# Sink attention: the order of scores, dense products and weighing in a cycle of two units, and the split of the PSUM banks

## The chip, the cores and the metric

The kernel runs on one core of a Trainium2 chip. The core has a matrix engine (TensorE, PE in the profile), three engines for elementwise work (VectorE or DVE, ScalarE or ACT, GpSimd or POOL), a queue for transfers (SyncE or SP), and the accumulation memory PSUM, into which PE writes. The kernel uses PSUM as eight banks of 128 x 512 floats. The metric is the device time of one execution in microseconds; the median of three executions is 4220.33 us (4219.34 to 4223.46).

## The reference

The program computes sixteen blocks of a small hybrid network, each of them as `x = x + block(layernorm(x))`, over 16 sequences of 256 tokens with 128 channels. The change lies in one of them, attention with a sliding window of 128 tokens and a "sink": an extra score per head that takes part in the softmax but carries no value. Cut to what matters:

```
h = layernorm(x);  n = rmsnorm(h, scale)
q = rope(n Wq + bq), k = rope(n Wk + bk)    # 16 query heads, 4 key heads, 64 wide
v = n Wv + bv
scores = q . k where |pos_q - pos_k| <= 128, else a very low number
probs = softmax([scores, sink]) without the last column
h = h + (probs v) Wo + bo
```

The kernel doesn't take the maximum away before the exponential. So a head's output is (sum of exp(score) v) / (sum of exp(score) + exp(sink)), and everything in it is a matrix product, an exponential, a mask, or a division. A mixture of experts follows in the same block.

## The kernel before

The stage is `window_attention` of the class `Fast` (from line 3190). The 4096 tokens are eight chunks of 512, each holding two sequences of 256. A unit of the attention is (chunk c, side, sequence b, query tile it, key tile jt), with tiles of 128 tokens and a side being half of the heads; there are 8 x 2 x 2 x 2 x 2 = 128 units, and two neighbours with jt = 0 and 1 make the weighted sums of one query tile. What happens to unit n:

- `score(n)` (line 3249) takes two score banks, `self.bank("s")`, and issues two matmuls of 512 columns on PE, one on SBUF rows 0 to 63 and one on rows 64 to 127. ACT takes the exponential of both banks into the tile `pt` (128 x 1024).
- `masked(n)`: where it and jt differ, DVE multiplies `pt` with the mask `far`. For jt = 1, POOL adds the pair's two `pt` tiles to `both`, from which the denominators come.
- `weigh(n, slot)` (line 3272): for each unit, eight matmuls `pt` x `v` of 128 rows by 32 columns into four quarters of the bank `po`; for jt = 1 also four matmuls of ones x `both` into the bank `pd`, the denominators. Each of these lines' matmuls leaves two records in the trace.
- `inverse`: ACT takes the logarithm of `pd` plus the sink's exponential, in two halves, and then exp of its negative, which is the reciprocal `rd`. The two logarithms release `pd`.
- `divide`: DVE multiplies `po` with `rd` into `ot`, and so releases `po`.

Around this, the same loop issues dense products on PE, with the full 128 x 128 array: `prepare` projects q, k and v of the next side (eight slots ahead of its first unit; each roped projection is read from PSUM by two DVE instructions, then shuffled by DVE and added by POOL at the next step), `out` is the output projection of four matmuls, and `before` and `after` are the norms of the next and the last chunk. From the second chunk on the norms have a compact form, in which line 1798 makes four small matmuls of 128 rows by 32 columns, ACT takes two functions of the result, and SP sends the rows out with four small transfers. Each dense product takes one bank of the tag "s" and gives it back when DVE or ACT has read it.

The order is written out by hand (`manual_schedule`), by a loop over slots n. Every slot has one score unit. An even slot goes on with dense products (`prepare`, `out`, `before`, `after`), an odd slot with `weigh` of the units n - 3 and n - 2. A dictionary `due` holds what is deferred to the beginning of a later slot, after the slot's score: `masked(n)` in slot n + 1, `inverse` in the slot after its weighing, `divide` one later, and the `peak` reductions of DVE.

`share` splits the eight PSUM banks among tags; a tag's banks are used in turn, and an allocation waits until the bank's last user is read out. Before, four banks are "s" (scores and dense products together) and four are "o" (`po` and `pd` in turn).

Of the kernel before, what the change touches and what calls it, by code (L numbers as in the profile page):

```python
# [1649 lines left out]
class Fast(Net):  # L1650
# [1539 lines left out]
    def window_attention(self, w, h, n1, ns2):  # L3190
# [3 lines left out]
        with ExitStack() as st:  # L3194
# [7 lines left out]
            units = [(c, side, b, it, jt) for c in range(NCH) for side in range(2) for b in range(2) for it in range(2) for jt in range(2)]  # L3202
            qs, ks, vs, pts, ots, sums, both, due = {}, {}, {}, {}, {}, {}, {}, {}
# [19 lines left out]
            def later(slot, f, *args):  # L3223
                due.setdefault(slot, []).append((f, args))

            def prepare(i, step, slot):

                c, side = divmod(i, 2)
                s = self.chunk(c)
                while pending:  # L3230
                    moved()
                if step == 0:
                    qs[i] = p2.tile([P, 4, CH], F32, tag="q", name="q")
                    ks[i] = p2.tile([P, CH], F32, tag="k", name="k")
                    roped("k", side, s, ks[i])
                    later(("last", slot + 4), self.peak, WINDOW + side, 1, c, ks[i])
                for g in ((0,), (1, 2), (3,), ())[step]:
                    roped("q", 4 * side + g, s, qs[i][:, g])
                    later(("last", slot + 4), self.peak, WINDOW + side, 0, 4 * c + g, qs[i][:, g])
                if side == 0 and step > 1:  # L3240
                    pv = self.bank("s")
                    v = p1.tile([P, 2, T], F32, tag="v", name="v", bufs=4)
                    for k in range(2):
                        t = 2 * step - 4 + k
                        self.mm(pv[:, k * T : k * T + T], n1[:, c * CH + t * P : c * CH + t * P + P], w["Wv"])
                        vs[c, t] = v[:, k]
                    self.tt(v, self.bt(pv), w["bv"][:, None, :].broadcast_to([P, 2, T]), ALU.add)

            def score(n):
                c, side, b, it, jt = units[n]  # L3250
                i0, j0 = b * T + it * P, b * T + jt * P
                q, k = qs[2 * c + side], ks[2 * c + side]
                pt = p2.tile([P, 2, 4, P], F32, tag="pt", name="pt", bufs=6)
                ps = [self.bank("s"), self.bank("s")]
                for half in range(2):
                    rows = slice(64 * half, 64 * half + 64)
                    self.mm(ps[half].rearrange("p (h t) -> p h t", h=4), k[rows, j0 : j0 + P], q[rows, :, i0 : i0 + P])
                for half in range(2):
                    self.act(pt[:, half].rearrange("p h t -> p (h t)"), ps[half], AF.Exp)
                pts[n] = pt  # L3260
# [11 lines left out]
            def weigh(n, slot):  # L3272
                c, side, b, it, jt = units[n]
                if jt == 0:
                    sums[0] = self.bank("o"), self.bank("o")
                pt = pts.pop(n)
                po, pd = sums[0]


                for dh in range(3 if jt else 2):  # L3280
                    if dh == 2:
                        pt = both.pop(n)
                    for r in range(4):
                        half, hh = divmod(r, 2)
                        d = (2 * side + half) * 64 + 32 * dh
                        at = dh % 2 * T
                        nc.tensor.matmul(
                            (pd if dh == 2 else po)[32 * r : 32 * r + 32, at : at + T],
                            self.ones64[:, :32] if dh == 2 else vs[c, 2 * b + jt][:, d : d + 32],
                            pt[:, half, 2 * hh : 2 * hh + 2].rearrange("p h t -> p (h t)"),  # L3290
                            start=dh == 2 or (jt == 0 and dh == 0), stop=dh == 2 or (jt == 1 and dh == 1), skip_group_check=True,
                        )
                if jt:
                    later(slot + 1, inverse, n, po, pd, slot + 2)
# [19 lines left out]
            def out(i):  # L3314
                c, side = divmod(i, 2)
                pz = self.bank("s")
                ot = ots.pop(i)
                for g in range(4):
                    at = (4 * side + g) * C
                    self.mm(pz, w["Wof"][:, at : at + C], ot[:, g], start=g == 0, stop=g == 3)  # L3320
                hs = h[:, self.chunk(c)]
                if side:
                    self.tt(hs, hs, pz, ALU.add)
                else:
                    self.stt(hs, pz, w["bo"], hs, ALU.add, ALU.add)
# [3 lines left out]
            def before(c, i):  # L3329

                s = self.chunk(c)
                if i == 0:
                    held["sq"] = self.centre_step(p1, self.x[:, s], h[:, s], "s", square=True)
                elif i == 1:
                    held["rs"] = self.spread_step(p1, held["sq"], "s", twice=True, compact=c > 0)
                else:
                    r1, r2 = held["rs"]
                    self.stt(n1[:, s], h[:, s], w["ns1"], r2, ALU.mult, ALU.mult)
                    self.tt(h[:, s], h[:, s], r1, ALU.mult)

            def after(c, i):

                s = self.chunk(c)
                if i == 0:
                    held["sq"] = p1.tile([P, CH], F32, tag="nsq", name="nsq", bufs=2)
                    self.act(held["sq"], h[:, s], AF.Square)
                elif i == 1:
                    held["rs"] = self.spread_step(p1, held["sq"], "s", compact=c < NCH - 1)
                else:
                    self.stt(n1[:, s], h[:, s], ns2, held["rs"], ALU.mult, ALU.mult)  # L3350

            with self.share(s=4, o=4), self.tc.manual_schedule():
                self.logs()
                for n in range(-14, len(units) + 16):
                    if 0 <= n < len(units):
                        score(n)
                        later(n + 1, masked, n)
                    for f, args in (*due.pop(n, []), *due.pop(("last", n), [])):
                        f(*args)
                    if n % 2:  # L3360
                        for i in (n - 3, n - 2):
                            if 0 <= i < len(units):
                                weigh(i, n)
                        continue
                    i, step = divmod(n + 8, 8)
                    if 0 <= i < 2 * NCH:
                        prepare(i, step // 2, n)
                    i, rest = divmod(n - 14, 8)
                    if rest == 0 and 0 <= i < 2 * NCH:
                        out(i)  # L3370
                    c, u = divmod(n + 16, 16)
                    if c == 0 and u in (2, 4, 6):
                        before(c, u // 2 - 1)
                    if u in (0, 2, 6) and 0 < c < NCH:
                        before(c, (u + 1) // 3)
                    c, u = divmod(n - 24, 16)
                    if u in (0, 2, 6 if c < NCH - 1 else 4) and 0 <= c < NCH:
                        after(c, (u + 1) // 3 + (u == 4))
# [497 lines left out]
```

## Time and profile before

| | |
|---|---|
| median of three runs | 4220.33 us |
| profiled execution | 4218.15 us, its span 4216.4 us |
| PE busy, whole span | 3831.5 us (91%) |
| DVE, ACT, POOL busy, whole span | 2551.0, 2281.8, 1853.7 us |
| this stage, from its first projection to its last products | about 2881.9 to 3347 us from the span's start |
| one chunk of the stage in its steady part | 56.6 us |
| PE, DVE, ACT, POOL busy in it | 56.60, 45.47, 28.16, 31.29 us |

How to read it: one execution is recorded by the hardware profiler. A row of the timeline gives the start from the span's start, the length of the merged instructions, the engine, the line of the kernel, the operation, "what it writes <- what it reads", the shape, and how many records were merged; brackets give the idle time of the engine before it and what ended it. Most matmuls are issued in a helper at line 504, so the tiles' names tell them apart: `ps<-q,k` is a score, `ps<-hb,w`, `ps<-w,hb` and `ps<-ot,w` are dense products, `ps<-pt,v` of line 3287 is the weighing and `ps<-both,ct` the denominators. The shape before the sizes (64\*128, 128\*128, 128\*32) is the part of the array that the matmul uses. The ends of matmuls are modelled by the profiler, so starts are the safer reading.

### The profile page before, as it was taken

The page shows a single profiled execution, that of the slowest core. Times are in us where ns is not written, and L with a number is a line of the kernel's source. Part 1 is how long each engine was busy: PE and PEld are TensorE (multiplying, and loading weights), DVE is VectorE, ACT ScalarE, POOL GpSimd, SP SyncE. Part 2 cuts the span into 40 slices and gives each one's busy share as a digit, 9 for nine tenths or more (in the row PEclk, how much of TensorE's full clock was granted, in tenths as well). Part 3 has the DMA queues.
Part 4 walks back from the last instruction along what each step waited for, and adds up shares of the span by engine and source line. Part 5 has one row for each costly group of instructions (what it writes and reads, how often), then busy time and mean ns, then how long its engine had stood idle before and what let it go on. Part 6 is the DMA issues. An engine that isn't in the chain of part 4 may idle for free. (4 is left out here: it accounts for less than half of the span.)

```text
span 4216.4 us, 74153 instructions
## 1 busy us (share of the span) xinstructions
PE 3831.5 (91%) x29030; PEld 2182.7 (52%) x29030; DVE 2551.0 (61%) x4503; ACT 2281.8 (54%) x4478; POOL 1853.7 (44%) x1632
## 2 busy tenths in 40 slices
PE   7999999998899999985989869888999999899978
PEld 3555466464455466454965459543444344455333
DVE  4776576374577477473346633556877676486474
ACT  6665466555766466652457634444554454774532
POOL 4754365232565166225433434454555455321251
PEclk8999999998999999996999979999999999999979
DMA  1800000000000000004920058100000000000000
GB/s 61 347 15 12 11 9 9 22 1 1 20 11 14 6 7 9 6 11 142 323 69 12 17 182 295 41 19 21 16 14 16 8 0 10 7 2 19 6 0 21
DMA packets 110086, 190.88 MB, mean 45 GB/s; under 512 B 16126, under 2 KB 70788, under 8 KB 109600
## 3 DMA queue, kind: packets, MB, share of 16 engines
q1 hardware_dynamic: 97248, 162.83, 11.7%
q0 software_dynamic: 9120, 18.51, 1.3%
q8 instruction: 231, 3.78, 0.4%
q10 hardware_dynamic: 3360, 4.72, 0.3%
q14 instruction: 127, 1.04, 0.1%
HBM read 118.28 MB, written 54.20 MB: 41 GB/s over the span
## 5 line engine op out<-in xcount | busy, mean ns | idle before, releaser
L528 ACT ACTIVATE pt<-ps 128x512 f32<-128x512 f32 x640 | 339.5, 600 | 337.5 <-PE ps L504 336.2
L504 PE MATMUL ps<-hb,w 128*128 128x512 f32 (+1 forms) x960 | 463.7, 617 | 3.9 <-issue 3.3
L504 PE MATMUL ps<-w,hb 128*128 128x512 f32 (+2 forms) x896 | 405.2, 573 | 27.3 <-DVE t L531 18.5
L534 POOL TENSOR_TENSOR t<-t,t 128x512 f32<-128x512 f32 x256 | 319.9, 1271 | 153.7 <-DVE t L531 107.8
L531 DVE TENSOR_TENSOR t<-ps,tab 128x512 f32<-128x512 f32 x512 | 317.5, 681 | 70.1 <-ACT sq L528 66.7
L534 POOL TENSOR_TENSOR t<-t,ss 128x1024 f32<-128x1024 f32 x128 | 243.7, 1904 | 195.2 <-ACT ss L528 194.0
L504 PEld LDWEIGHTS ps<-hb,w 128*128 128x128 f32 (+1 forms) x960 | 179.6, 191 | 261.8 <-issue 220.6
L528 ACT ACTIVATE qkt<-ps 128x512 f32<-128x512 f32 x256 | 140.6, 595 | 299.2 <-PE ps L508 299.2
L531 DVE TENSOR_TENSOR u<-u,ps 128x384 f32<-128x384 f32 (+1 forms) x206 | 121.8, 595 | 277.2 <-ACT u L528 114.9
L534 POOL TENSOR_TENSOR nsq<-ha 128x512 f32<-128x512 f32 x112 | 123.2, 1100 | 354.3 <-ACT ha L528 342.3
L531 DVE TENSOR_TENSOR ot<-ps,rd 128x512 f32<-128x512 f32 (+2 forms) x224 | 143.2, 639 | 209.8 <-ACT rd L528 209.8
L504 PEld LDWEIGHTS ps<-w,hb 128*128 128x128 f32 x896 | 154.1, 193 | 174.4 <-issue 111.7
L534 POOL TENSOR_TENSOR both<-pt 128x1024 f32<-128x1024 f32 x64 | 151.2, 2363 | 199.0 <-DVE pt L531 191.3
L504 PE MATMUL ps<-ot,w 128*128 128x512 f32 x448 | 213.6, 611 | 17.4 <-DVE ot L531 9.9
L504 PE MATMUL ps<-xt,w 128*128 128x128 f32 x1704 | 221.0, 280 | 1.6 <-ACT xt L528 1.5
L2225 POOL DMA_INDIRECT back<-y,x x142 | 139.1, 980 | 186.1 <-ACT y L528 69.5
L504 PE MATMUL ps<-u,w 128*128 128x512 f32 (+1 forms) x448 | 215.4, 605 | 3.4 <-POOL u L534 3.4
L504 PEld LDWEIGHTS ps<-xt,w 128*128 128x128 f32 x1704 | 204.5, 194 | 3.4 <-ACT xt L528 3.4
L528 ACT ACTIVATE u<-ps,w 128x512 f32<-128x512 f32 x160 | 107.7, 685 | 173.3 <-PE ps L504 170.6
L3479 PE MATMUL ps<-qkt 64*128 64x192 f32 (+1 forms) x2048 | 181.8, 311 | 9.6 <-ACT rd L528 9.6
L504 PE MATMUL ps<-ha,w 128*128 128x512 f32 x320 | 176.1, 672 | 11.6 <-ACT f L528 10.2
L504 PE MATMUL ps<-nsq,ct 128*128 128x512 f32 x272 | 154.5, 652 | 30.8 <-POOL nsq L534 26.6
(366 smaller groups left out, 8756.2 us busy)
## 6 DMA issues: line engine op xcount, KB each, us to landing
w<-in_moe_x SPq DMA_DIRECT2D x142, 533.0 KB
rows<-t SPq DMA_DIRECT2D x64, 520.0 KB
nrs<-nrow SPq DMA_DIRECT2D x220, 64.0 KB
x<-rows SPq DMA_DIRECT2D x142, 65.0 KB
w<-in_local_f SPq DMA_DIRECT2D x8, 659.5 KB
y<-back ACTq DMA_DIRECT2D x16, 256.0 KB
y<-back SPq DMA_DIRECT2D x16, 256.0 KB
w<-in_local_f SPq DMA_DIRECT2D x4, 658.5 KB
```

Source lines behind the costliest of these rows:

```text
L504: self.nc.tensor.matmul(out, lhsT, rhs, start=start, stop=stop)
L528: self.nc.scalar.activation(out, in_, func, **kw)
L531: self.nc.vector.tensor_tensor(out, a, b, op)
L534: self.nc.gpsimd.tensor_tensor(out, a, b, op)
L2225: nc.gpsimd.indirect_dma_start(views[i], bass.IndirectOffsetOnAxis(ap=x[:, C : C + 1].bitcast(I32), axis=0), y, None, bounds_check=2 * NT ...
L3479: nc.tensor.matmul(out, kt[rows, g, t * P : t * P + P], qt[rows, g, t * P : t * P + wide], start=(i, t) == (0, 0), stop=i == 1, skip_group ...
```

## The change

Two things change. In the loop over slots, an even slot now issues the scores of both its own unit and the next one, and odd slots issue none; `masked` of both is deferred to the next even slot, ahead of the weighing of these units in the odd slot after it. The cycle of two slots is thus score, score, dense products, weighing, where it was score, dense products, score, weighing. And the PSUM banks are split anew: five for "s", two for "o", which now holds `po` alone, and one for the new tag "d", which holds `pd`.

```diff
             def weigh(n, slot):
                 c, side, b, it, jt = units[n]
                 if jt == 0:
-                    sums[0] = self.bank("o"), self.bank("o")
+                    sums[0] = self.bank("o"), self.bank("d")
...
-            with self.share(s=4, o=4), self.tc.manual_schedule():
+            with self.share(s=5, o=2, d=1), self.tc.manual_schedule():
                 self.logs()
                 for n in range(-14, len(units) + 16):
-                    if 0 <= n < len(units):
-                        score(n)
-                        later(n + 1, masked, n)
+                    if n % 2 == 0 and 0 <= n < len(units):
+                        for i in (n, n + 1):
+                            score(i)
+                            later(n + 2, masked, i)
                     for f, args in (*due.pop(n, []), *due.pop(("last", n), [])):
                         f(*args)
                     if n % 2:
                         for i in (n - 3, n - 2):
                             if 0 <= i < len(units):
                                 weigh(i, n)
                         continue
```

## The prediction

> **What bounds the kernel now.** I read the page first: TensorE (PE) is busy 91% of the span; the chain that ended last covers only some 6% of it, at the end of the program, and says nothing of this stage. Then the busy times of one chunk of the sink attention, taken from one score run to the same one a chunk later:
>
> ```profile
> core 0: us, PE busy (x) PEld busy (x) DVE busy (x) ACT busy (x) POOL busy (x), PEclk, DMA share, GB/s
> 3019.96:3076.57 56.61, 56.61 (x451) 23.36 (x447) 45.51 (x74) 28.16 (x64) 31.31 (x19) 1.00 0.07 15
> ```
>
> PE has no idle time in 56.61 us, at full granted clock; VectorE (DVE) has 20% to spare, ScalarE (ACT) half. The chunk is PE's list. Next PE's timeline in that chunk (start, length, line, tiles, shape, count of records; one matmul leaves two records):
>
> ```profile
> 3036.70 0.61 PE L3287 MATMUL ps<-both,ct 128*32 128x256 f32 x8
> 3037.24 1.13 PE L504 MATMUL ps<-q,k 64*128 64x512 f32 x4
> 3038.30 1.98 PE L504 MATMUL ps<-hb,w 128*128 128x512 f32 x4
> 3040.22 1.13 PE L504 MATMUL ps<-q,k 64*128 64x512 f32 x4
> 3041.28 1.93 PE L3287 MATMUL ps<-pt,v 128*32 128x256 f32 x32
> 3043.03 0.61 PE L3287 MATMUL ps<-both,ct 128*32 128x256 f32 x8
> 3043.57 1.13 PE L504 MATMUL ps<-q,k 64*128 64x512 f32 x4
> 3044.63 1.98 PE L504 MATMUL ps<-hb,w 128*128 128x512 f32 x4
> 3046.55 0.43 PE L1798 MATMUL ps<-nsq,ct 128*32 128x128 f32 x8
> 3046.90 1.68 PE L504 MATMUL ps<-q,k 64*128 64x512 f32 x4
> 3048.51 1.93 PE L3287 MATMUL ps<-pt,v 128*32 128x256 f32 x32
> ```
>
> Read starts, not lengths. One cycle of two units is: scores (S, rows 64), dense (D, 128*128), scores, weighing (W, 128*32), denominators (Wb, same shape). Dense records follow each other at 0.427. Two score matmuls, on different halves of the rows, run together: 0.853 of streaming. But the next run always starts 1.06 after S (3037.24 to 3038.30), and 1.92 after four dense records that stream 1.707 (3038.30 to 3040.22). So each change of array shape costs 0.206. W to Wb, without a change, costs 1.75 less 1.707 = 0.044; Wb to S 0.545 less 0.427 = 0.118. The S of 3046.90 takes 1.61, not 1.06: 0.55 of waiting for a score bank, as its second half's weights start 0.56 late; the score run before the first weighing of each chunk (3019.96 to 3021.43) waits 0.41 likewise. At the stage's end, where no dense work stands between, the trace already has the run that the change makes:
>
> ```profile
> 3318.67 1.99 PE L504 MATMUL ps<-q,k 64*128 64x512 f32 x8
> 3320.58 1.93 PE L3287 MATMUL ps<-pt,v 128*32 128x256 f32 x32
> ```
>
> Two units' scores in 1.91 instead of twice 1.06: 0.206 less, no wait inside. Last, who waits for whom in this stage, and the other engines' timeline:
>
> ```profile
> ACT pt L528 <- PE ps L504: 205.5, 102, 3.4
> POOL both L534 <- DVE pt L531: 191.3, 61, 10.1
> ```
> ```profile
> 3052.03 1.09 ACT L528 ACTIVATE pt<-ps 128x512 f32<-128x512 f32 x2 [2.81 <-PE ps L504]
> 3053.00 0.64 ACT L528 ACTIVATE rd<-ps,es 128x128 f32<-128x128 f32 x2
> 3056.06 1.23 DVE L531 TENSOR_TENSOR pt<-pt,w 128x1024 f32<-128x1024 f32 x1 [0.43 <-ACT pt L528]
> 3057.43 2.36 POOL L534 TENSOR_TENSOR both<-pt 128x1024 f32<-128x1024 f32 x1 [2.42 <-DVE pt L531]
> ```
>
> ACT and GpSimd (POOL) wait for work, not PE for them. This sum of `both` ends at 3059.79, and PE uses it at 3065.50: through a steady chunk it is 3.3 to 5.7 us early.
>
> **The change, part by part.**
>
> *One shape change less per cycle.* Before: S-D, D-S, S-W, Wb-S. After: S-D, D-W, Wb-S. D-W is not in the trace, but D to line 1798's 128*32 matmul is (3044.63 to 3046.55: 1.92, so 0.206). Six of a chunk's eight cycles: 6 x 0.206 = 1.24.
>
> *The two cycles with a compact norm (V, line 1798) between D and S.* Before: V-S 0.356 less 0.213 = 0.143, then S-W 0.206. After: V-W, both 128*32. Not in the trace; between 0.044 (as W-Wb) and 0.206 (as any change). I take 0.044, the same shape: 0.305 each, 0.61 per chunk; with the other end 0.29.
>
> *The two waits for a score bank*, 0.41 + 0.55 = 0.96 per chunk, go, if five banks serve. Replay with t = 0 at the score run's start. A score run's exps start 1.22 after it (3050.81 to 3052.03), 0.49 apart, so four of them run from 1.22 to 3.3. The first D takes the fifth bank at 1.92. The second D, at 2.77, needs the first exp's bank, free at 1.82: 0.95 early. The third, at 3.6, needs the next: 1.3 early. The next cycle's scores need the last exp banks and the first dense ones, which DVE reads; that is over a weighing (2.3 us) later, so more than 1 us early. No wait.
>
> *One bank for denominators.* Its release is the two Ln on ACT (0.64), now behind four exps: about 3.3 + 0.6 = 3.85 (before, two pd banks gave a cycle more). Wb comes at 1.92 + D + 0.206 + 1.75, with one D product 4.73: 0.9 early. With no D at all, which happens only in the ends of the stage, it comes at 3.67 and waits 0.2.
>
> *Masking and `both` one slot later.* The cycle's mask and the sum now both stand at the head of the slot of the dense work; the exps that they read are a cycle old, so they begin when DVE gets there. DVE's list in the heaviest cycle (mask 1.23, two shuffles 1.26, four evictions 2.64, two peaks 1.27, division 0.68) is 7.1, against PE's 1.92 + 1.71 + 0.21 + 1.75 + 0.55 = 6.13; two such cycles follow each other, so DVE falls up to 1.9 behind, and lighter ones give it back (chunk: 45.5 of 53.8). `both` is ready at lag + 1.23 + 2.36 + 0.2 = lag + 3.8, Wb comes at 5.58: early by 1.8 to about 0. This is the thinnest cover; I take no wait, and 0.3 in a quarter of the cycles (5 us in all) as the other end. Behind a late Wb stands PE's whole queue, next the following score run.
>
> No instruction, eviction or DMA is added; the row DMAs of the norm (SP) stay in their slots, behind nothing new.
>
> **A rule against it.** The Trainium skill, "TensorEngine Tiling (Array Packing)", section PSUM Bottleneck, warns that faster matmuls may leave the PSUM copy as the bottleneck. Here four score banks fill in 1.71 while ACT needs 4 x 0.49 = 1.96 after its 1.22 lead. If PE had to stand until the last exp (3.3) before dense work, a cycle would lose 3.3 - 1.92 = 1.4, 64 of them 88 us: 4290. The rows speak against: the dense run in between asks one bank at a time, the first free, the second 0.95 early. I go by the rows. For the price of a change, the page "TensorE: Matmul & The Clock Gate", Single matmul latency, puts the drain at about 175 ns; by that estimate the six changes save 1.05 instead of 1.24 a chunk, 1.5 us less in all. The measured 0.206 is used.
>
> **Sum.** A steady chunk: 1.24 + 0.61 + 0.96 = 2.81, to 53.8 us. Seven periods from the first unit's scores to the last chunk's: 19.7. The last chunk has fewer D (one cycle only V, two nothing): about 5 x 0.206 + 0.75 = 1.8 saved, but three or four cycles have no cover (0.2 for the denominators, 0.15 + lag for `both`), some 2 to 3 us; the first cycles are similarly thin. Both ends together: -1 (from -3 to +2). In all 18.7. The profiled execution took 4218.15 (span 4216.4 and 1.75 around it): 4199.5. The median of the runs is 2.2 above it: **4201.6 us**.
>
> **Rivals.**
> - *A smaller gain* (8%): V-W costs a full change (-2.2), `both` late in a quarter of the cycles (-5), or a bank wait comes back (-3): 4206 to 4211. For it: DVE's two heavy cycles. Against: 0.8 or more to spare in most.
> - *No change* (6%): the new order turns the spared changes into waits in the same place, say each cycle 0.3 for `both`: 18.7 - 19.2, about 4221. For it: S-W waits of 0.41 and 0.55 show that PE already meets its banks. Against: these come from four banks, now five.
> - *Slower* (8%): the chain mask, `both`, Wb becomes the stage's bound. Place: Wb in the 32 cycles with two roped projections. Price: if masks run 1.53 each (as one at 3048.44 beside POOL's work) and DVE's lag grows to where Wb stands 1 us in each of these, 32 us: 4201.6 + 32 = 4234. It decides from 18.7 / 32 = 0.58 per heavy cycle, and is measurably slower from 0.85. For it: POOL's 191 us of waiting for this mask. Against: that was idle time, with 3.3 to 5.7 to spare of which the change uses 2 to 3.
>
> **How the numbers follow.** A measurement tells about 0.2%, 8.4 us, from no change: faster is below 4211.9, slower above 4228.8. The likeliest case (78%) has 4195 to 4208. Its best: ends at +2 and D-W as cheap as V-S (0.143, so 0.063 x 6 x 7.5 = 2.8 more): 19.7 + 2 + 2.8 = 24.5, so 4195.8. Its worst: ends at -3, V-W at 0.206 (-2.3) and the runs' own scatter of 2: 12.4, so 4208. Faster: 78 + 8 = 86%; same 6%; slower 8%. The range takes the likeliest case and most of the smaller gain: 4195 to 4210.
>
> **What would show it.** After: PE's timeline with score runs of x8 in every cycle, the next run 1.91 to 1.92 later; D to W 0.206 over its streaming; line 1798 to W about 0.26; a chunk of 53.8; no score run longer than 1.92; Wb 1.75 after W. Wrong would be Wb starting later than 1.8 after W (which of pd and `both` released it tells the rivals apart), dense records with gaps inside the run after x8 scores (banks), or DVE near 100% in a chunk.

## The result and the profile after

The changed kernel takes 4204.58 us in the median of seven runs (4196.97 to 4209.55), the kernel before 4220.33 us (4218.32 to 4223.46); the ratio is 0.9956, with a 95% interval of 0.9947 to 0.9965. It is 15.75 us faster; 18.7 were forecast, and the measured time lies inside the range given.

The busy times of one steady chunk of the stage in the changed kernel; the window is 53.76 us long because that is the distance from one weighing to the same one a chunk later (it was 56.60):

```profile
core 0: us, PE busy (x) PEld busy (x) DVE busy (x) ACT busy (x) POOL busy (x), PEclk, DMA share, GB/s
3053.76:3107.52 53.76, 53.76 (x447) 23.59 (x446) 45.15 (x74) 27.34 (x65) 31.29 (x19) 1.00 0.07 16
```

PE is still without idle time at full clock. DVE and POOL are busy for about as long as before (45.15 and 31.29 us, where it was 45.51 and 31.31), in a chunk that is 2.84 us shorter. PE's timeline in the changed kernel:

```profile
3037.53 1.99 PE L504 MATMUL ps<-q,k 64*128 64x512 f32 x8
3039.45 1.98 PE L504 MATMUL ps<-hb,w 128*128 128x512 f32 x4
3041.36 1.93 PE L3287 MATMUL ps<-pt,v 128*32 128x256 f32 x32
3043.11 0.61 PE L3287 MATMUL ps<-both,ct 128*32 128x256 f32 x8
3043.66 1.99 PE L504 MATMUL ps<-q,k 64*128 64x512 f32 x8
3045.58 1.98 PE L504 MATMUL ps<-hb,w 128*128 128x512 f32 x4
3047.49 0.43 PE L1798 MATMUL ps<-nsq,ct 128*32 128x128 f32 x8
3047.73 1.91 PE L3287 MATMUL ps<-pt,v 128*32 128x256 f32 x32
3049.46 0.61 PE L3287 MATMUL ps<-both,ct 128*32 128x256 f32 x8
```

Both units' scores take 1.92 from start to start, never more in the steady part. Dense to weighing is 1.91 over 1.707 of streaming, the 0.206 that was taken for it. The compact norm to the weighing takes 0.242 over 0.213 of streaming (3047.49 to 3047.73): 0.03, as good as nothing; both use the same shape. The denominators (Wb) start 1.75 after the weighing (W), so they wait neither for `both` nor for a bank.

Where the time went, from the starts of PE's matmuls in the two profiles (us):

| stretch of the stage | before | after | saved |
|---|---|---|---|
| first score run to first weighing | 13.01 | 11.56 | 1.45 |
| weighings of the first chunk | 53.23 | 53.87 | -0.64 |
| the next five chunks, each | 56.60 | 53.76 | 2.84 |
| the seventh | 55.00 | 52.66 | 2.34 |
| first weighing of the eighth to the last output product | 41.97 | 43.04 | -1.07 |
| the stage from its first score run | 446.23 | 429.91 | 16.3 |

The two profiled executions differ by 4216.4 - 4202.7 = 13.7 us of span, not by 16.3. The rest lies outside the stage, where no instruction was changed: 4.4 us were lost before it and 1.8 gained behind it. Two stretches far ahead of the stage, in the kernel before:

```profile
830.00:850.00 20.00, 18.11 (x167) 14.72 (x167) 14.08 (x29) 6.66 (x9) 6.97 (x9) 0.81 0.19 75
850.00:870.00 20.00, 19.13 (x184) 13.37 (x182) 16.02 (x36) 12.51 (x20) 7.93 (x9) 0.93 0.00 1
```

and the same two in the changed one:

```profile
830.00:850.00 20.00, 18.30 (x137) 15.32 (x130) 13.07 (x27) 6.89 (x9) 6.33 (x7) 0.59 0.06 23
850.00:870.00 20.00, 20.00 (x168) 14.93 (x168) 12.92 (x28) 9.25 (x15) 6.29 (x7) 0.67 0.00 1
```

The third number from the right is the granted clock of PE: 0.81 and 0.93 against 0.59 and 0.67. By the starts of the same instructions, the changed kernel is 2.4 us ahead at 815 us and 8.3 us behind at 880 us. So it falls back by 10.7 us there, of which it later makes up a part. It is not put down to the change: a second profile of the changed kernel has 0.70 and 0.70 in these stretches, and a kernel with the new order alone 0.79 and 0.91. What sets this clock is not shown. Because executions of one kernel on one chip differ by up to 23 us, and the chips by 1%, the experiments are read from the stage in their profiles, where a chunk repeats within 0.01 us, and by the ratio to the kernel before on the same chip.

### The profile page after: what moved, and what is told of

It reads as the page before. It is cut to its first block, busy times and chain, and to the rows that moved or that the text cites. A ratio compares the mean times of both kernels' runs of the same rounds, so it can differ in the third digit from the quotient of the medians.

```text
span 4202.7 us, 74216 instructions
## 1 busy us (share of the span) xinstructions
PE 3807.1 (91%) x29030; PEld 2187.5 (52%) x29030; DVE 2546.4 (61%) x4503; ACT 2279.2 (54%) x4478; POOL 1853.1 (44%) x1632
```

## The experiments

Theory A: PE is the bound of the stage and each change of array shape costs it 0.206 us; the order spares one per cycle, and the waits for score banks go as well. Theory B: the banks, above all the fifth one, are the gain. A further question is how thin the cover of `both` is (the slower rival). In the table, "stage" is the time from the first score run to the last output product, "chunk" the steady one, both in us and from one profile each; "dense split" is the kernel in which a fourth shape change is put back.

| kernel | chunk | stage | ratio to before, same chip |
|---|---|---|---|
| before | 56.60 | 446.23 | 1 |
| whole change | 53.76 | 429.91 | 0.9956 (0.9947 to 0.9965) |
| the same again | 53.76 | 429.91 | 0.9962 (0.9946 to 0.9977) |
| order alone | 53.76 | 429.77 | 0.9967 (0.9954 to 0.9979) |
| split of banks alone | 55.64 | 439.85 | 0.9986 (0.9977 to 0.9994) |
| masks early | 53.76 | 428.90 | 0.9969 (0.9956 to 0.9981) |
| masks late | 59.44 | 471.33 | 1.0063 (1.0047 to 1.008) |
| dense split | 55.81 | 444.87 | 1.0 (0.9992 to 1.0008) |
| dense split, masks early | 54.55 | 432.43 | one execution, no interval |
| masks early, two and two | 53.76 | 428.70 | one execution, no interval |
| the same, peaks late | 53.76 | 428.23 | 0.9958 (0.9944 to 0.9971) |

**The order alone.**

```diff
-                    sums[0] = self.bank("o"), self.bank("d")
+                    sums[0] = self.bank("o"), self.bank("o")
-            with self.share(s=5, o=2, d=1), self.tc.manual_schedule():
+            with self.share(s=4, o=4), self.tc.manual_schedule():
```

> Only the new order; the banks stay four for scores and dense products and four for the two results. Theory A (the order is the gain; a shape change of TensorE costs 0.206 us): a steady chunk of 53.8 us as with the whole change, since the first dense product needs the bank of the first score half, whose exponential ends 1.82 us after the score run's start, and it starts at 1.92; at most 0.1 us of wait per cycle, so the chunk lies between 53.8 and 54.6. Theory B (the fifth bank took the two waits of 0.41 and 0.55 away): the chunk keeps them and is 54.7 or more, and a score run of eight records is followed by its next run later than 1.92.

The chunk is 53.76, to the hundredth that of the whole change, and the stage 0.14 us shorter. PE's timeline of this kernel:

```profile
3000.97 1.99 PE L504 MATMUL ps<-q,k 64*128 64x512 f32 x8
3002.89 1.12 PE L504 MATMUL ps<-hb,w 128*128 128x512 f32 x2
3003.85 1.03 PE L504 MATMUL ps<-w,hb 128*128 128x256 f32 x4
3004.81 1.93 PE L3287 MATMUL ps<-pt,v 128*32 128x256 f32 x32
```

With four banks, the first dense product needs the bank of the first score half, and it still starts 1.92 after the scores: that exponential has ended 0.1 before. Theory B falls, for the new order. The rows also say how to read the price of a change: each of the two dense tensors here takes 0.96, that is 0.107 over its 0.853 of streaming, and only the whole dense stretch shows the 0.206 (1.92 over 1.707). A stretch of one tensor takes the same 1.92, so a second tensor of the same shape costs nothing more.

**The split alone.** The old order of the loop with five, two and one banks.

> Only the new split of the banks (five, two, one); the order is the old one. Theory A: no shape change is spared, only the two waits of 0.41 and 0.55 can go: chunk 55.6 us, some 7 us less in all than before. If the waits are not a matter of the count of banks but of the order (theory C), they stay and the chunk is 56.6. Theory B (all of the gain is from the banks): chunk near 53.8.

A chunk is 55.64: 0.96 less than before, the two waits of 0.41 and 0.55. The profile of this kernel shows the place of the second one:

```profile
3007.50 0.43 PE L1798 MATMUL ps<-nsq,ct 128*32 128x128 f32 x8
3007.85 1.13 PE L504 MATMUL ps<-q,k 64*128 64x512 f32 x4
3008.91 1.93 PE L3287 MATMUL ps<-pt,v 128*32 128x256 f32 x32
```

1.06 from scores to weighing, where it was 1.61; the first one, 1.47 before, is 1.06 too. So either part takes these waits away, and the two gains don't add: of the chunk's 2.84, the order alone gives all, the split alone 0.96. What only the order gives is 1.88 per chunk.

**A fourth shape change put back, with the scores left together.** In the first two dense slots of a side, the second roped projection goes behind the weighing.

```diff
-                    roped("q", 4 * side + g, s, qs[i][:, g])
+                    if step < 2 and g in (0, 2) and slot >= 0:
+                        behind.append((4 * side + g, s, qs[i][:, g]))
+                    else:
+                        roped("q", 4 * side + g, s, qs[i][:, g])
...
                                 weigh(i, n)
+                        while behind:
+                            roped("q", *behind.pop(0))
```

> The whole change, but in the first two dense slots of each side (30 of the 64 cycles) the second roped projection goes behind the weighing: scores of both units, one or more dense products, weighing, one dense product. Scores stay together; only a fourth shape change comes back in these cycles (weighing to dense and dense to scores in place of weighing to scores). Theory A (a shape change costs its 0.206 wherever it stands): such a cycle is 0.15 to 0.25 us longer, four of them per chunk: 54.3 to 54.8 instead of 53.76, some 6 us in all. Rival (the gain is from scores standing together, not from the count of changes): chunk stays at 53.76. Waits for the pair's sum may add up to 0.3 per chunk, since the weighing comes 0.85 earlier in these cycles, where the sum has 1.85 to spare.

The chunk came to 55.81, 2.05 more than the whole change, over what was expected. PE's timeline of it:

```profile
3054.52 1.91 PE L3290 MATMUL ps<-pt,v 128*32 128x256 f32 x32
3056.58 0.64 PE L3290 MATMUL ps<-both,ct 128*32 128x256 f32 x8 [0.15 <-POOL both L534]
3057.15 1.12 PE L504 MATMUL ps<-hb,w 128*128 128x512 f32 x2
3058.20 1.99 PE L504 MATMUL ps<-q,k 64*128 64x512 f32 x8
```

Wb stands 2.06 after W, not 1.75, and its row names `both`: the weighing comes earlier in these cycles than the sum. Over the steady chunks the start of Wb after W averages 1.894, where it was 1.748, so 0.146 x 8 = 1.17 of the 2.05 are waits. Most of the rest is the shape change: Wb to dense takes 0.55 to 0.57, about as Wb to scores did (0.545), and dense to scores 1.055 over 0.853 of streaming: 0.2 more, four times. To see that part alone, the masks were put one slot earlier as well:

> The kernel with the second projection behind the weighing in 30 cycles, whose chunk was 55.81: its profile shows 0.118 from denominators to dense and 0.206 from dense to scores in place of 0.118 from denominators to scores, four times a chunk (0.83), and 1.19 per chunk of waiting for the pair's sum. Here the masks stand one slot earlier, which gives the sum 0.6 us more. If the account is right, the 0.83 stays and most of the 1.19 goes: chunk 54.6 to 54.9. If the price of the fourth shape change were smaller than 0.2, the chunk would come nearer to 53.76.

The chunk is 54.55, and Wb averages 1.745 after W, so no wait is left: 0.79 over 53.76 in four cycles, 0.20 for each shape change. PE's timeline of one such cycle:

```profile
3013.77 0.61 PE L3290 MATMUL ps<-both,ct 128*32 128x256 f32 x8
3014.32 1.13 PE L504 MATMUL ps<-hb,w 128*128 128x512 f32 x2
3015.37 1.99 PE L504 MATMUL ps<-q,k 64*128 64x512 f32 x8
3017.29 1.12 PE L504 MATMUL ps<-hb,w 128*128 128x512 f32 x2
```

That settles theory A against the thought that scores are cheaper when they stand together: they stand together here too. What PE does in these 0.2 us the runs don't show.

**Masks earlier.**

```diff
-                            later(n + 2, masked, i)
+                            later(n + 1, masked, i)
```

> The whole change, with the masks and the sum of the pair one slot earlier, ahead of the division in VectorE's order. Theory (in the steady part the sum has 0.98 to 4.4 us to spare, only the stage's ends wait for it): steady chunk unchanged at 53.76; every distance between the end of the sum and the denominators that use it grows by up to 0.6 us; of the waits at the ends (1.27 at the fourth weighing, some 0.2 three times and about 0.8 at the last, 0.94 for the mask at the last weighing) 1 to 2.5 us go. Rival (steady part has hidden waits for the sum): the chunk itself gets shorter than 53.6.

The chunk does not move. In the whole change the sum ends 0.98 to 4.45 us ahead of its use in a steady chunk; here it is 1.6 to 5.06. The stage is 1.0 us shorter, at the lower end of what was expected: it is the end of the stage that gains (43.04 to 42.10). In the first chunk the wait at the third weighing stayed, a little shorter (Wb 2.83 after W, where it was 3.02).

**Masks later.** The masks and sums run behind the slot's peaks and shuffles. Here `moved` issues the shuffles, and `masks` runs what is deferred to the slot under the key "mask". Cut to what matters:

```diff
                 while pending:
                     moved()
+                masks(slot)
...
-                            later(n + 2, masked, i)
+                            later(("mask", n + 2), masked, i)
...
                     if 0 <= i < 2 * NCH:
                         prepare(i, step // 2, n)
+                    masks(n)
```

> The whole change, with the masks and the sum put behind the slot's peaks and shuffles in VectorE's order, so 0.6 to 2.5 us later in a cycle and behind the additions on GpSimd. Theory (the cover of the sum is thin, 0.98 to 1.86 us in five cycles of eight): waits of 1 to 4 us per chunk at the denominators, a chunk of 54.8 to 57.8, in all 8 to 32 us slower than the whole change: the upper half of that is slower than before. Rival (the sum has ample cover): chunk 53.8, no loss.

A chunk is 59.44, and the kernel is 1.0063 of the kernel before: slower, though every shape change is still spared. This is the prediction's slower rival, brought about by the place of the masks; the loss went over what was expected. The timeline of this kernel shows why:

```profile
3054.48 1.89 DVE L531 TENSOR_TENSOR pt<-pt,w 128x1024 f32<-128x1024 f32 x1
3055.25 2.27 POOL L534 TENSOR_TENSOR q<-q,t 128x512 f32<-128x512 f32 x1
...
3056.42 1.93 PE L3292 MATMUL ps<-pt,v 128*32 128x256 f32 x32 [1.01 <-DVE pt L531]
...
3057.48 2.36 POOL L534 TENSOR_TENSOR both<-pt 128x1024 f32<-128x1024 f32 x1
...
3059.89 0.64 PE L3292 MATMUL ps<-both,ct 128*32 128x256 f32 x8 [1.53 <-POOL both L534]
```

The mask (1.2 alone) takes 1.9 and POOL's addition (1.28 alone) 2.27 where the two overlap; the sum stands behind both. PE stands 1.0 for the mask before the weighing and 1.5 for the sum behind it. In this order the mask falls just where POOL adds. The two causes, the later place and the overlap, were not separated; as an estimate, the overlap delays this sum by about 1 us, by which the addition is longer (2.27 less 1.28).

**Two ways past the whole change.** First, masks early with four banks for scores and dense products, two for `po`, two for `pd`:

> New order with the masks one slot earlier, and banks four for scores and dense products, two for sums, two for denominators. The steady chunk stays at 53.76; against the early masks alone the waits for a single denominators' bank in the cycles without dense work at the stage's end go: 0.2 to 0.6 us in all, stage 428.3 to 428.8.

428.70, inside what was expected. Then the first side's peak reductions also later, `slot + (4 if i else 10)` in place of `slot + 4`:

> As the one before, and the first side's five peak reductions wait ten slots instead of four, so that they don't stand between the first projections on VectorE. The first score run, which waits for GpSimd's last addition and so for VectorE's shuffles, comes 1.5 to 2.4 us earlier after the first projection (16.65 before), the chunks stay at 53.76, and the stage from first projection to last output product is some 4 us shorter than with the whole change as it is. Rival: VectorE's list at the stage's start is not what the first scores wait for, and nothing moves.

The first score run comes 14.29 us after the first projection instead of 16.65, 2.36 earlier. In the kernel before and in the kernel without this step (16.67), DVE's list has four of these reductions (0.6 each) ahead of the last shuffle that it waits for; here it has none. From first projection to last output product this is 442.52 against 446.56 for the whole change (446.56 = 16.65 + 429.91): 4.0 us less. In the times of whole executions it can't be told from the whole change (0.9958 beside 0.9962), so it is better in the stage's profile only.

**The same again.**

> The whole change once more, beside the parts on one chip. Stage as in the first profile of it: chunk 53.76, first score run to last output product 429.9 us. The rest of the program may differ by up to 10 us with the clock granted at 830 to 900 us from the start.

Its chunk and its stage repeat to 0.01 us.

## Why the prediction was right, and what was mis-sized

- *One shape change less per cycle, 0.206, 1.24 a chunk*: right, and shown from the other side by putting one back (0.20).
- *The norm next to the weighing*: 0.044 was taken, 0.03 was measured; the other end, 0.206, is excluded.
- *The two bank waits, 0.96*: they went, as summed. But the condition given, "if five banks serve", was not needed: the order alone takes them away with four. Under the new order the fifth bank, and with it the single denominators' bank, bought nothing.
- *A chunk of 53.8*: 53.76.
- *One bank for denominators*: 0.93 to 4.4 us early in every steady cycle, where 0.9 was worked out for the thinnest.
- *Thin cover of `both`, from 1.8 to about 0*: it was 1.85 in the heaviest cycles, which were replayed, and 0.98 in the thinnest, so no wait. That the change lives on this cover was right: a shift of the masks within the same slot made it slower than before.
- *The sum's ends were mis-sized.* Seven periods (19.7) and both ends together (-1, from -3 to +2) made 18.7. The measured sum of all periods and ends is 16.3, so 3.4 of the 19.7 were lost where 1 was put. The first period (up to the second chunk's first weighing) saves 0.81, 2.0 short of the 2.81 put for it; the seventh chunk saves 2.34, 0.5 short; the last chunk loses 1.07; the five steady ones give 0.15 more. For the last chunk the sum's own terms hold (1.8 saved, 2 to 3 lost without cover):

```profile
3327.78 1.93 PE L3287 MATMUL ps<-pt,v 128*32 128x256 f32 x32 [0.94 <-DVE pt L531]
3330.32 0.64 PE L3287 MATMUL ps<-both,ct 128*32 128x256 f32 x8 [0.60 <-POOL both L534]
```

The last weighing waits 0.94 for its mask, its denominators come 0.8 late, and three earlier ones 0.2 to 0.3 late: 2.5 in all. It is the start, put down only as "similarly thin", that was mis-sized. There two things came: the wait for `both`, which was named, and behind it a drop of the clock, which was not. PE's timeline at the start of the stage after the change:

```profile
2923.98 1.93 PE L3287 MATMUL ps<-pt,v 128*32 128x256 f32 x32
2927.00 0.64 PE L3287 MATMUL ps<-both,ct 128*32 128x256 f32 x8 [1.08 <-POOL both L534]
2928.67 3.55 PE L504 MATMUL ps<-q,k 64*128 64x512 f32 x8 [1.03 <-POOL q L534]
2932.15 1.98 PE L504 MATMUL ps<-hb,w 128*128 128x512 f32 x4
```

Wb is 3.02 after W, 1.27 late. The next scores then take 3.48 from start to start instead of 1.92. The windows around it show the clock (third number from the right):

```profile
2925.00:2928.40 3.40, 1.55 (x28) 0.42 (x17) 3.37 (x6) 1.28 (x4) 3.40 (x2) 1.00 0.00 0
2928.40:2931.90 3.50, 3.23 (x8) 1.18 (x8) 3.10 (x4) 1.09 (x2) 1.05 (x2) 0.51 0.02 5
```

PE was busy 1.55 of 3.40 us in the first window, and got half the clock in the next: a further 1.56 us. The second profile of this kernel and that of the order alone show the same there (3.47 and 3.49). In the kernel before, where Wb is 0.24 late at this weighing, the stage's clock is at full rate from 2906 on without such a dip.

With the stage's 16.3 in place of 18.7 the forecast would have been 4204.0; the measured median is 4204.58. That the two agree so closely is partly luck, as the executions spread over 12.6 us.

## What to carry to other kernels

Where PE never idles, count its changes of array shape and price them from start-to-start distances in the trace: runs of one shape put together pay about 0.2 us for each change spared, even if no engine does less work. Then replay what each moved producer still has to spare, since the same order with the masks a few instructions later was slower than before. And count the steady periods separately from a loop's two ends: a gain that needs other work as cover isn't had there.

## What the runs showed of the hardware

- A shape change cost 0.206 us over the streaming of the whole stretch before it, from 64\*128 or from 128\*128 to another shape, but 0.118 from the weighing's 128\*32 to scores or to dense work, and 0.143 from the compact norm to scores; between two tensors of the same 128\*32 shape 0.03 to 0.044.
- A wait can cost more than its own length. Two stops of PE of little more than 1 us each, in one stretch of 3.4 us, were followed by 3.5 us at half clock. The Trainium skill's page "TensorE: Matmul & The Clock Gate", section Why this matters for your kernels, warns of idle gaps of over some 3 us; here shorter ones came before the drop. But it is no rule: in the kernel with the dense split the first of these stops is longer (1.46 by its row, where it was 1.08), the second as long (1.03), and the clock stays full:

```profile
2929.80:2933.22 3.42, 0.93 (x16) 0.16 (x8) 3.39 (x5) 0.44 (x2) 3.37 (x2) 1.00 0.00 0
2933.22:2936.60 3.38, 3.38 (x18) 1.27 (x22) 3.12 (x5) 2.22 (x6) 0.98 (x1) 1.00 0.02 5
```

At the end of the stage in the changed kernel, too, PE is busy 0.88 of 3.40 us and the next 3.40 have full clock. So that the stops brought the drop about is likely, not shown, and which stops do is open.
- A DVE product of two tensors in SBUF and a POOL addition lengthen each other when they overlap: 1.2 to 1.9, and 1.28 to 2.27. The skill's "SBUF — State Buffer", section Who interferes with whom, says that a DVE instruction with two SBUF inputs contends with POOL's reads, and the rows agree in that both are longer; so the price of a mask depends on where it falls in time.
